# A third level of the seven-product scheme, in one of the seven inner products, in a two-layer LoRA kernel

## Chip, cores and metric

The kernel runs on one core of one Trainium2 chip. The metric is the device time in microseconds of one execution of the whole program. The time before the change is 521.71 us, the median of three runs (521.3 to 521.96).

## The reference, cut to what matters

All arrays are float32. `x` has 64 requests of 64 tokens with 1024 features, 4096 tokens in all.

```python
# layer 0: a rank-16 adapter per request, added to x
Bx  = einsum('bni,bri->bnr', x, B0[ids0])
x   = x + einsum('bnr,bor->bno', Bx, A0[ids0])
# layer 1: a dense 1024 x 1024 product and eight gated adapters of rank 16, added to x
base   = einsum('btd,od->bto', x, W)
logits = einsum('btd,ed->bte', x, Wr) + 5.0 * one_hot(ids1)
gates  = softmax over the two largest logits, zero elsewhere
h      = einsum('btd,erd->bter', x, A1)
x      = x + base + 2.0 * einsum('bter,bte,eor->bto', h, gates, B1)
```

Nearly all the arithmetic is `base`, the product of 4096 tokens with the 1024 x 1024 matrix `W`. The `x +` of layer 1 is folded into it, as an identity added to `W`.

## The kernel before

**Layout and stages.** Features lie on the partitions, tokens along the free axis. The 4096 tokens are eight blocks of 512 (`TB`), worked off as four pairs (`NSUP`; the pair is called `s`, 0 to 3). For each block there are a few small TensorE stages: transposes of gathered adapter rows (`pt`), the projection to rank 16 (`project`, tile `pb` written from `x,bt`), the rank-16 update of x (`adapt`, tiles `px`, added to x on VectorE), the adapters and router logits (`rows`, tile `ph`, 128 x 136 per matmul), the gates (VectorE) and a transpose of the gated rows (`pg`, line 609). The rest is the dense product.

**The dense product** (`products`, line 817) is done twice over with the Strassen-Winograd scheme, which gets a 2 x 2 by 2 x 2 block product from seven block products instead of eight, at the price of sums of blocks. The outer level takes the two feature halves, the two output halves and the two token blocks of a pair: seven outer products, n = 1, 2, 6, 7, 5, 3, 4 in that order (`ORDER`, line 251). The inner level splits each outer product (512 features, 512 outputs, 512 tokens) again into seven inner products k = 1 to 7, each of 256 features, 256 outputs and 256 tokens. One inner product is four matmul instructions of 128 x 128 weights and 256 tokens (`product`, line 876): two output halves, each summed over two feature halves. In n = 2, 3, 7 and 4, four of the inner products (k = 2, 3, 7, 4) carry two more matmuls, which add the gated adapters from `b1_sb`. Only outer product 1 of pair 0 is done without the inner split (`WHOLE`, tile `pw`).

**Operands.** For pair 0 the weight sums of the inner level are made by GpSimd (`weights`, line 700) and written to DRAM (`s_kept`); the pairs 1 to 3 read all seven weight tiles of an outer product back through SP's queue, into the rotating SBUF pool `"s"` of 28 tiles, 256 KB each. Token sums of the outer level are made by VectorE (`token_sum`, line 736), those of the inner level by GpSimd in pairs 1 to 3 (`inner_tokens`, line 758).

**PSUM and leaving it.** Pools `"a"` and `"b"` have two banks each, `"l"` four. Products 1, 6, 5 and 3 of an outer product add up in one bank `pa`, 7 and 4 in one bank `pb2`, and product 2 is alone in a bank `pc` of pool `"b"` (all shown as `pb` in the profile). `leave` (line 909) takes a bank out after each step, while the sum goes on in it: VectorE adds it to the output tile, or ScalarE copies it where there is nothing to add. So a later step into the same bank waits for the `leave` of the step ahead of it.

**Order of the work.** Inside `products` each outer product does `step(n, 1)`, the left-over steps 3 and 4 of the outer product before it in between, `step(n, 2)`, then `begin` of the next outer product, then 6, 7 and 5. Each operation is a step of a planner (`Plan`, line 34) with a cost on its engine, a due time `at`, what it reads and writes and which pool slots it takes. The planner lists the steps in time once, when the program is built, and each engine runs its own list strictly in that order, with semaphores between engines. All instructions go out through one wrapper, so the profile shows line 29 for nearly all of them, and groups are told apart by tile names.

Of the kernel before, what the change touches and what calls it, by code (L numbers as in the profile page):

```python
# [8 lines left out]
F32 = mybir.dt.float32  # L9
I32 = mybir.dt.int32  # L10
AF = mybir.ActivationFunctionType
ALU = mybir.AluOpType
AX = mybir.AxisListType

P = 128
# [166 lines left out]
def kernel(  # L182
# [59 lines left out]
    QC = NC // 4  # L242
    QO = O // 4
    HT = TB // 2
# [8 lines left out]

    WHOLE = {(0, 1)}

    pe, dve = Pinned(tc, nc.tensor), Pinned(tc, nc.vector)
    act, pool, sp = Pinned(tc, nc.scalar), Pinned(tc, nc.gpsimd), Pinned(tc, nc.sync)
    engine = {"DVE": dve, "POOL": pool}

    slots = {  # L260
        "q": 7, "s": 28, "t5": 2, "t6": 2, "t7": 2, "t4": 2, "o": 3, "hg": 3, "hd": 3,
        "gb": 2, "ga": 2, "bt": 1, "bx": 1, "h": 1, "l": 4, "a": 2, "b": 2,
    }
    plan = Plan(slots, {"l"})
# [7 lines left out]
    def new(tag, shape, name):  # L272
        return pools[tag].tile(shape, F32, tag=tag, name=name)
# [36 lines left out]
    b1_sb = const.tile([P, O], F32, name="b1_sb")  # L310
# [44 lines left out]
    made = {}  # L355

    def part(t, cs=range(HC), gs=range(NG)):
        return [(t, c, g) for c in cs for g in gs]
# [302 lines left out]
    }  # L661
    m_q = {1: quarter[0, 0], 2: quarter[0, 1], 4: quarter[1, 1]}
    s_kept = tc.dram_tile([7, 7, P, QC * QO], F32, name="s_kept")

    def combine(out, a, b, op, at, engines):

# [9 lines left out]
    DVE = {"DVE": 0.62}  # L676
    POOL = {"POOL": 1.25}
# [20 lines left out]
    wt, ti = {}, {}  # L698

    def weights(s, n, at):  # L700

        out = {}
        if s > 0:
            for i, m in enumerate(ORDER):
                out[m] = t = ("s", s, n, m)

                def fn(e, t=t, m=m):
                    made[t] = new("s", [P, QC, QO], f"s_{s}_{n}{m}")
                    sp.dma_start(made[t].rearrange("p c o -> p (c o)"), s_kept[n - 1, m - 1])

                plan.add({"SP": 0.1}, fn, [("kept", n, m)], [(t,)], at + i - 8, [("s", t)], kb=256)
            wt[n] = out
            return
        m = m_q[n]
        out = {1: m[0, 0], 2: m[0, 1], 4: m[1, 1]}
        for k, (u, v, op) in {
            5: ((1, 0), (1, 1), ALU.add),
            6: (5, (0, 0), ALU.subtract),
            7: ((0, 0), (1, 0), ALU.subtract),
            3: ((0, 1), 6, ALU.subtract),  # L720
        }.items():
            out[k] = ("s", s, n, k)
            uu = m[u] if isinstance(u, tuple) else out[u]
            vv = m[v] if isinstance(v, tuple) else out[v]
            combine(out[k], uu, vv, op, at - 4, POOL)
        for k in ORDER:
            t = out[k]

            def keep(e, t=t, k=k):
                sp.dma_start(s_kept[n - 1, k - 1], made[t].rearrange("p c o -> p (c o)"))  # L730

            plan.add({"SP": 0.1}, keep, [(t,)], [("kept", n, k)], at + 4, kb=256)
        wt[n] = out


    def token_sum(s, n, at):
# [21 lines left out]
    def inner_tokens(s, n, m, at):  # L758
        def b(i, j):
            return made[m][:, i * QC : (i + 1) * QC, j * HT : (j + 1) * HT]  # L760

        def keys(i, j):
            return part(m, range(i * QC, (i + 1) * QC), range(2 * j, 2 * j + 2))

        out = {k: (("view", i, j), keys(i, j)) for k, i, j in ((1, 0, 0), (2, 1, 0), (3, 1, 1))}
        for k, u, v in ((5, (0, 1), (0, 0)), (6, (1, 1), 5), (7, (1, 1), (0, 1)), (4, (1, 0), 6)):
            t = ("ti", s, n, k)

            def fn(e, t=t, k=k, u=u, v=v):
                made[t] = new(f"t{k}", [P, QC, HT], f"ti_{s}_{n}{k}")  # L770
                vv = b(*v) if isinstance(v, tuple) else made["ti", s, n, v]
                engine[e].tensor_tensor(made[t], b(*u), vv, ALU.subtract)

            vk = keys(*v) if isinstance(v, tuple) else [(("ti", s, n, v),)]
            plan.add(
                POOL if s else DVE, fn, keys(*u) + vk, [(t,)], at - 5,
                [(f"t{k}", t)], sb=True,
            )
            out[k] = (t, [(t,)])
        ti[n] = {  # L780
            k: ((lambda t=t: b(*t[1:])) if t[0] == "view" else (lambda t=t: made[t]), ks)
            for k, (t, ks) in out.items()
        }
# [33 lines left out]
    def products(s):  # L817
        ka, kb = 2 * s, 2 * s + 1
        slot = [0]
        hd, dest, banks, left = {}, {1: "U", 6: "U", 7: "V"}, {}, {}  # L820
# [7 lines left out]
        def at():  # L828
            return s * SLOTS + slot[0]
# [5 lines left out]
        def q(d, i, cs, js):  # L835
            t = made[d][i] if isinstance(d, str) else made["o", s, d, i]
            return t[:, cs[0] : cs[-1] + 1, js[0] * HT : (js[-1] + 1) * HT]

        def qk(d, i, cs, js):
            return [(name(d, i), c, j) for c in cs for j in js]  # L840

        ALL = (0, 1)
# [66 lines left out]
        def leave(n, ps, i, cs, js, more=False):  # L909
# [22 lines left out]
                [("o", name(d, i))] * fresh,  # L932
            )

        def done(n, i, cs, js):

            if n == 5:

                p5, u, v = (lambda d=d: q(d, i, cs, js) for d in (5, "U", "V"))
                k5, ku, kv = (qk(d, i, cs, js) for d in (5, "U", "V"))  # L940
                plan.add(
                    DVE, lambda e: dve.tensor_tensor(u(), u(), p5(), ALU.add), ku + k5, ku,
                    at() - 2, sb=True,
                )
                plan.add(
                    DVE, lambda e: dve.tensor_tensor(p5(), v(), p5(), ALU.add), kv + k5, k5,
                    at() - 2, sb=True,
                )
            oh, k = {2: (0, ka), 5: (1, kb), 3: (0, kb), 4: (1, ka)}.get(n, (None, None))
            if oh is None:  # L950
                return
            o0 = (oh * 2 + i) * QO
            if last(n):


                def some(e):
                    t0, r0 = k * TB + js[0] * HT, o0 + cs[0] * P
                    sp.dma_start(
                        outT[r0 : r0 + len(cs) * P, t0 : t0 + HT].rearrange("(c p) t -> p c t", p=P),
                        q(n, i, cs, js),  # L960
                    )

                plan.add({"SP": 0.1}, some, qk(n, i, cs, js), [], at() + 2, kb=128 * len(cs))
                return
            left[n, i] = left.get((n, i), 2) - 1
            if left[n, i] == 0:

                def store(e):
                    sp.dma_start(
                        outT[o0 : o0 + QO, k * TB : (k + 1) * TB].rearrange("(c p) t -> p c t", p=P),  # L970
                        made["o", s, n, i],
                    )

                plan.add({"SP": 0.1}, store, qk(n, i, ALL, ALL), [], at() + 2, kb=512)

        def begin(n):
            dest.setdefault(n, n)
            if s == 0 and n in (6, 3):
                outer(n, at() - 4)
            weights(s, n, at() + (6 if (s, n) in WHOLE else 0))  # L980
            if s == 0 and n == 2:
                outer(5, at() + 4)
                outer(7, at() + 8)
            if (s, n) in WHOLE:
                whole_h[n] = {2: ("hg", ka), 3: ("hg", kb), 7: ("hg", kb), 4: ("he", s)}.get(n)
                if n == 4:
                    gate_diff(s, at() - 2)
                return
            inner_tokens(s, n, tokens[n], at())
            if n == 4:  # L990
                gate_diff(s, at() - 2)
            if n in (2, 7, 3, 4):
                gate_sum(s, n, hd, at() - 2)
# [34 lines left out]
        for n in ORDER:  # L1028
            after = ORDER[ORDER.index(n) + 1] if n != ORDER[-1] else None
            if (s, n) in WHOLE:  # L1030
                for k in rest:
                    step(*k)
                rest = []
                for x in range(4):
                    whole_product(n, x // 2, x % 2)
                    if x == 1 and after is not None:
                        begin(after)
                continue
            step(n, 1)
            if rest:  # L1040
                step(*rest[0])
            step(n, 2)
            if rest:
                step(*rest[1])
            if after is not None:
                begin(after)
            step(n, 6)
            step(n, 7)
            step(n, 5)
            rest = [(n, 4), (n, 3)] if last(n) else [(n, 3), (n, 4)]  # L1050
        for k in rest:
            step(*k)
# [89 lines left out]
```

## Time and profile before

| | |
|---|---|
| median of three runs | 521.71 us (521.3 to 521.96) |
| the profiled execution, its own time | 521.43 us |
| span of that execution in the profile | 519.6 us |
| granted TensorE clock, mean | 1.0 |
| ScalarE copy `h<-ph`, 272 columns, x16 | 386 ns each |
| ScalarE copy `o<-pa`, 512 columns, x16 | 586 ns each |
| VectorE `bx<-pb,mask`, 128 columns, x8 | 286 ns each |
| VectorE `hd<-hg`, 256 columns, x8 | 420 ns each |
| VectorE `o<-pb,o`, 512 columns, x47 | 690 ns each |
| GpSimd `ti<-x`, 512 columns, x24 | 1283 ns each |
| DMA, mean over the span | 191 GB/s, 99.19 MB in packets |

Times in the profile count from the start of the span. PE is TensorE's matmul row and PEld its weight loads, which overlap it. A float32 matmul instruction stands as two records, each with a weight load of its own: the 256 instructions of `ph` (8 blocks, 4 strips, 8 chunks) are 512 records. A transpose is one record. The length of a record includes the pipeline's fill and drain, so the rate of a run of matmuls is read from start to start, not from the mean length. A timeline line gives start, length, engine, line, operation, output<-inputs, shape, how many records in a row, and in brackets how long the engine idled before it and what released it.

### The profile page before, as it was taken

Reading aid. Unit: us, or ns where it says so; the run is one execution under the profiler, and the core shown is the slowest. Engines: PE = TensorE matmul, PEld = TensorE weight load, DVE = VectorE, ACT = ScalarE, POOL = GpSimd, SP = SyncE. Lnnn points to the kernel's source line nnn. Section 1 sums busy time; section 2 is a strip of 40 time slices with the busy share of each in tenths; the row PEclk is TensorE's granted clock in tenths of the full one; section 3 lists DMA queues with packets and bytes.
Section 4 is the critical chain, followed back from the end, with each engine's and each line's share of the span. In section 5 each row is a group of like instructions: output and inputs, shape, how many; then the busy total and the mean of one; then the engine's idle time right before and its main releaser. Section 6 shows DMA issues by size and latency. Waiting matters only on the chain.

```text
span 519.6 us, 8547 instructions
## 1 busy us (share of the span) xinstructions
PE 505.6 (97%) x3432; PEld 439.8 (85%) x3432; DVE 301.2 (58%) x574; ACT 41.0 (8%) x81; POOL 170.2 (33%) x141
## 2 busy tenths in 40 slices
PE   2999999999999999999999999999999999999997
PEld 2857988888888988898888998889888898888886
DVE  0689998986853383616693256345576417433633
ACT  1111100002000100012000100000200010000000
POOL 4073058180332144123243313311423322433300
PEclk9999999999999999999999999999999999999999
DMA  7999275799666259726575536743546634620122
GB/s 263 371 368 400 78 262 216 272 326 350 199 187 218 61 179 317 242 74 204 165 241 168 177 86 214 266 166 109 174 163 199 203 88 112 208 65 0 42 101 101
DMA packets 54263, 99.19 MB, mean 191 GB/s; under 512 B 4944, under 2 KB 11088, under 8 KB 54224
## 3 DMA queue, kind: packets, MB, share of 16 engines
q1 hardware_dynamic: 51920, 90.26, 52.3%
q0 software_dynamic: 2304, 8.39, 4.6%
q8 instruction: 27, 0.44, 0.3%
q14 instruction: 12, 0.10, 0.0%
HBM read 69.01 MB, written 29.62 MB: 190 GB/s over the span
## 4 chain that ended last, share of the span: by engine, by line
PE 97%; DMA 2%; DVE 0%; issue 0%; SPq 0%; POOL 0%
PE pa L29 39%; PE pb L29 38%; PE ph L29 11%; PE px L29 3%; PE pw L29 3%; DMA x<-in_xT 2%; PE pt L29 1%; PE pg L29 1%; DVE o L29 0%; SPq L29 0%; DVE bx L29 0%; POOL x L29 0%
## 5 line engine op out<-in xcount | busy, mean ns | idle before, releaser
L29 PE MATMUL pa<-ti,s 128*128 128x256 f32 x432 | 102.5, 380 | 0.0
L29 PE MATMUL pb<-ti,s 128*128 128x256 f32 x384 | 95.8, 380 | 0.0
L29 PEld LDWEIGHTS pa<-ti,s 128*128 128x128 f32 x432 | 80.8, 190 | 11.2 <-issue 0.2
L29 PEld LDWEIGHTS pb<-ti,s 128*128 128x128 f32 x384 | 72.1, 190 | 10.0
L29 PEld LDWEIGHTS ph<-a_sb,x 128*128 128x128 f32 x512 | 62.6, 190 | 1.5 <-issue 0.4
L29 PE MATMUL ph<-a_sb,x 128*128 128x136 f32 x512 | 63.1, 279 | 0.2 <-issue 0.2
L29 POOL TENSOR_TENSOR ti<-x,ti 128x512 f32<-128x512 f32 x24 | 32.2, 1340 | 78.0 <-PE pb L29 77.1
L29 DVE TENSOR_TENSOR o<-pb,o 128x512 f32<-128x512 f32 x47 | 32.4, 690 | 35.5 <-PE pb L29 21.1
L29 PE MATMUL pa<-x,s 128*128 128x256 f32 x216 | 51.9, 379 | 0.0
L29 POOL TENSOR_TENSOR ti<-t,ti 128x512 f32<-128x512 f32 x18 | 25.7, 1429 | 71.0 <-PE pb L29 61.3
L29 POOL TENSOR_TENSOR ti<-x 128x512 f32<-128x512 f32 x24 | 30.8, 1283 | 55.3 <-PE pb L29 41.8
L29 PEld LDWEIGHTS pa<-x,s 128*128 128x128 f32 x216 | 40.1, 190 | 5.3 <-issue 0.3
L29 DVE TENSOR_TENSOR x<-px,x 128x512 f32<-128x512 f32 x64 | 39.8, 682 | 7.2 <-PE px L29 7.2
L29 PE MATMUL pa<-t,s 128*128 128x256 f32 x168 | 41.0, 380 | 0.0
L29 POOL TENSOR_TENSOR ti<-t 128x512 f32<-128x512 f32 x18 | 24.4, 1357 | 42.9 <-PE pb L29 33.4
L29 PEld LDWEIGHTS pa<-t,s 128*128 128x128 f32 x168 | 31.6, 190 | 4.5 <-issue 0.4
L29 DVE TENSOR_TENSOR o<-pa,u 128x512 f32<-128x512 f32 x32 | 22.0, 688 | 20.7 <-PE pa L29 20.1
L29 POOL TENSOR_TENSOR s<-w,w 128x512 f32<-128x512 f32 x12 | 17.2, 1434 | 36.3 <-DVE w L29 36.3
L29 DVE TENSOR_TENSOR u<-pb,u 128x512 f32<-128x512 f32 x21 | 14.5, 689 | 25.1 <-ACT u L29 20.7
L29 PE MATMUL pb<-hg,b_sb 128*128 128x256 f32 x96 | 28.6, 379 | 0.0
L29 DVE TENSOR_TENSOR o<-pa,v 128x512 f32<-128x512 f32 x15 | 10.3, 689 | 24.0 <-PE pa L29 24.0
L29 DVE TENSOR_TENSOR v<-pa,u 128x512 f32<-128x512 f32 x16 | 11.0, 689 | 22.3 <-PE pa L29 22.1
(113 smaller groups left out, 611.0 us busy)
## 6 DMA issues: line engine op xcount, KB each, us to landing
s<-s_kept SPq DMA_DIRECT2D x147, 256.0 KB
x<-in_xT SPq DMA_DIRECT2D x15, 1024.0 KB
out_T<-o SPq DMA_DIRECT2D x30, 512.0 KB
s_kept<-s SPq DMA_DIRECT2D x28, 256.0 KB
s_kept<-w SPq DMA_DIRECT2D x18, 256.0 KB
w<-in_w SPq DMA_DIRECT2D x16, 256.0 KB
x<-in_xT SPq DMA_DIRECT2D x2, 512.0 KB
s_kept<-m SPq DMA_DIRECT2D x3, 256.0 KB
```

What stands on the lines that cost most here:

```text
L29: return self._tc.keep_in_program_order(f(*args, **kwargs))
```

## The change

From pair 1 on (`FINE = 1`), inner product k = 2 of every outer product is split a third time, by the same scheme: its 256 x 256 weights into four blocks of 128 x 128, its 256 tokens into two groups of 128. In place of four matmuls of 128 x 128 weights and 256 tokens there are seven of 128 x 128 weights and 128 tokens, in four parts. The first part does four of them, one into each quarter of the bank; the other three parts do one each, adding into the second quarter, and lie ahead of the steps 6, 7 and 5. Between the parts ScalarE copies the running second quarter into a new SBUF tile `cp` (after the first part, the fourth quarter as well). After the last part VectorE takes the bank out as before and makes three more additions, from `cp`.

The scheme needs sums of weight blocks (tile `sf`: four GpSimd operations of 128 columns per outer product in pair 1, kept in DRAM as `f_kept`, loaded by SP in pairs 2 and 3) and of token blocks (tile `tt`: three VectorE operations per outer product). Pool `"s"` goes from 28 tiles to 26 and now also holds `sf`. The two matmuls for the gated adapters stay as they are, behind the last part. Pair 0 does as before.

```diff
+    FINE = 1
-        "q": 7, "s": 28, "t5": 2, "t6": 2, "t7": 2, "t4": 2, "o": 3, "hg": 3, "hd": 3,
+        "q": 7, "s": 26, "tt": 2, "cp": 2, "t5": 2, "t6": 2, "t7": 2, "t4": 2, "o": 3, "hg": 3, "hd": 3,
+    f_kept = tc.dram_tile([7, P, QC * QO], F32, name="f_kept")
...
+    def fine_weights(s, n, a, at):
...
+            v.tensor_tensor(f[:, 0], a21, a22, ALU.add)
+            v.tensor_tensor(f[:, 1], f[:, 0], a11, ALU.subtract)
+            v.tensor_tensor(f[:, 2], a11, a21, ALU.subtract)
+            v.tensor_tensor(f[:, 3], a12, f[:, 1], ALU.subtract)
...
+        if s == FINE:
+            plan.add({"POOL": 1.6}, sums, [(a,)], [(t,)], at - 3, [("s", t)], sb=True)
+            plan.add({"SP": 0.1}, keep, [(t,)], [("fine", n)], at + 4, kb=256)
+        else:
+            plan.add({"SP": 0.1}, load, [("fine", n)], [(t,)], at - 6, [("s", t)], kb=256)
...
+        def begin_fine(n):
...
+                dve.tensor_tensor(
+                    f[:, :2], b[:, :, P:], b[:, 0, :].rearrange("p (h t) -> p h t", t=P), ALU.subtract
+                )
+                dve.tensor_tensor(f[:, 2], f[:, 1], b11, ALU.add)
+                dve.tensor_tensor(f[:, 3], b21, f[:, 2], ALU.subtract)
...
+        def fine_product(n, part_):
...
+                todo = [
+                    [(1, a11, b11), (0, a12, b21), (3, s3, t3), (2, a22, t4)],
+                    [(1, s2, t2)],
+                    [(1, s1, t1)],
+                    [(1, s4, b22)],
+                ][part_]
+                for x, (c, lhs, rhs) in enumerate(todo):
+                    pe.matmul(
+                        out[:, c], lhs, rhs, start=(part_ == 0 and x == 0), stop=True,
+                        skip_group_check=True,
+                    )
...
+            def copy(e):
...
+                    act.copy(made[cp][:, 0::3], out[:, 1::2])
+                else:
+                    act.copy(made[cp][:, part_], out[:, 1])
...
+            leave(n, ps, 0, ALL, (0,), True)
...
+            def rest_(e):
+                o, c = q(dest[n], 0, ALL, (0,)), made[cp]
+                c11, c21, c2 = o[:, 0, :P], o[:, 1, :P], o[:, 1]
+                dve.tensor_tensor(c11, c11, c[:, 0], ALU.add)
+                dve.tensor_tensor(c2, c2, c[:, 1:3].rearrange("p h t -> p (h t)"), ALU.add)
+                dve.tensor_tensor(c21, c21, c[:, 3], ALU.add)
...
-            step(n, 2)
+            if s >= FINE:
+                fine_product(n, 0)
+            else:
+                step(n, 2)
...
-            step(n, 6)
-            step(n, 7)
-            step(n, 5)
+
+            for x, k in enumerate((6, 7, 5)):
+                if s >= FINE:
+                    fine_product(n, 1 + x)
+                if s >= FINE and x == 2:
+                    done(n, 0, ALL, (0,))
+                step(n, k)
```

More of the change, by code (lines that the diff above doesn't have):

```diff
@@ L712, in weights @@
             wt[n] = out
+            if s >= FINE:
+                fine_weights(s, n, out[2], at)
             return
@@ L733, in weights, with blocks, load, sums @@
         wt[n] = out
+    def fine_weights(s, n, a, at):
+        t = ("sf", s, n)
+        def blocks():
+            made[t] = new("s", [P, QC, QO], f"sf_{s}_{n}")
+            return made[t].rearrange("p c (o w) -> p (c o) w", w=P)
+        def load(e):
+            blocks()
+            sp.dma_start(made[t].rearrange("p c o -> p (c o)"), f_kept[n - 1])
+        def sums(e):
+            f, w4 = blocks(), made[a].rearrange("p c (o w) -> p (c o) w", w=P)
+            a11, a21, a12, a22 = (w4[:, x] for x in range(4))
+            v = engine[e]
+            v.tensor_tensor(f[:, 0], a21, a22, ALU.add)
+            v.tensor_tensor(f[:, 1], f[:, 0], a11, ALU.subtract)
+            v.tensor_tensor(f[:, 2], a11, a21, ALU.subtract)
+            v.tensor_tensor(f[:, 3], a12, f[:, 1], ALU.subtract)
+        def keep(e):
+            sp.dma_start(f_kept[n - 1], made[t].rearrange("p c o -> p (c o)"))
+        if s == FINE:
[3 more added lines that the diff above has]
+            plan.add({"SP": 0.1}, load, [("fine", n)], [(t,)], at - 6, [("s", t)], kb=256)
+        wt[n]["fine"] = t
     def token_sum(s, n, at):
@@ L933, in leave, with fn @@
             )
+        fine = {}
+        def begin_fine(n):
+            t, (tx, tk) = ("tt", s, n), ti[n][2]
+            def fn(e):
+                made[t] = new("tt", [P, 4, P], f"tt_{s}_{n}")
+                f, b = made[t], tx()
+                b11, b21 = b[:, 0, :P], b[:, 1, :P]
+                dve.tensor_tensor(
[3 more added lines that the diff above has]
+                dve.tensor_tensor(f[:, 3], b21, f[:, 2], ALU.subtract)
+            plan.add({"DVE": 0.9}, fn, tk, [(t,)], at() - 3, [("tt", t)], sb=True)
@@ new lines, in fine_product, with fn @@
+        def fine_product(n, part_):
+            ps, cp = ("pc", s, n), ("cp", s, n)
+            a, f, t, (tx, tk) = wt[n][2], wt[n]["fine"], ("tt", s, n), ti[n][2]
+            extra = hd[n][2] if n in (2, 3, 7, 4) and part_ == 3 else None
+            oh = {2: 0, 3: 0, 7: 1, 4: 1}.get(n)
+            def fn(e):
+                if part_ == 0:
+                    made[ps] = new("b", [P, QC, HT], f"pf_{s}_{n}")
+                out = made[ps].rearrange("p o (h t) -> p (o h) t", t=P)
+                w4 = made[a].rearrange("p c (o w) -> p (c o) w", w=P)
+                a11, a21, a12, a22 = (w4[:, x] for x in range(4))
+                s1, s2, s3, s4 = (made[f].rearrange("p c (o w) -> p (c o) w", w=P)[:, x] for x in range(4))
+                b4 = tx()
+                b11, b21, b22 = b4[:, 0, :P], b4[:, 1, :P], b4[:, 1, P:]
+                t1, t3, t2, t4 = (made[t][:, x] for x in range(4))
+                todo = [
[9 more added lines that the diff above has]
+                    )
+                if extra is not None:
+                    for j in range(QC):
+                        o = oh * 2 * QC + j
+                        pe.matmul(
+                            made[ps][:, j], b1_sb[:, o * P : (o + 1) * P], extra[0](),
+                            start=False, stop=True, skip_group_check=True,
+                        )
+            reads = [(a,), (f,), (t,)] + tk + ([("b1",), extra[1]] if extra is not None else [])
+            plan.add(
+                {"PE": (0.88, 0.22, 0.22, 0.22)[part_] + 0.86 * (extra is not None)}, fn, reads,
+                [(ps,)], at(), [("b", ps)] * (part_ == 0),
+            )
+            slot[0] += (0.5, 0.13, 0.13, 0.13)[part_]
+            def copy(e):
+                out = made[ps].rearrange("p o (h t) -> p (o h) t", t=P)
+                if part_ == 0:
+                    made[cp] = new("cp", [P, 4, P], f"cp_{s}_{n}")
+                    act.copy(made[cp][:, 0::3], out[:, 1::2])
+                else:
+                    act.copy(made[cp][:, part_], out[:, 1])
+            if part_ < 3:
+                plan.add(
+                    {"ACT": 0.45 if part_ == 0 else 0.3}, copy, [(ps,)] + [(cp,)] * (part_ > 0),
+                    [(cp,)], at() - 4, [("cp", cp)] * (part_ == 0),
+                )
+                return
+            leave(n, ps, 0, ALL, (0,), True)
+            region = qk(dest[n], 0, ALL, (0,))
+            def rest_(e):
[4 more added lines that the diff above has]
+                dve.tensor_tensor(c21, c21, c[:, 3], ALU.add)
+            plan.add({"DVE": 0.9}, rest_, [(cp,)] + region, region, at() - 4, sb=True)
@@ L989, in begin @@
             inner_tokens(s, n, tokens[n], at())
+            if s >= FINE:
+                begin_fine(n)
             if n == 4:
@@ L1041, in products @@
                 step(*rest[0])
-            step(n, 2)
+            if s >= FINE:
+                fine_product(n, 0)
+            else:
+                step(n, 2)
             if rest:
@@ L1046, in products @@
                 begin(after)
-            step(n, 6)
-            step(n, 7)
-            step(n, 5)
+            for x, k in enumerate((6, 7, 5)):
+                if s >= FINE:
+                    fine_product(n, 1 + x)
+                if s >= FINE and x == 2:
+                    done(n, 0, ALL, (0,))
+                step(n, k)
             rest = [(n, 4), (n, 3)] if last(n) else [(n, 3), (n, 4)]
```

## Prediction

> **What bounds the kernel.** I read the busy table of the page first, then what the matmul engine waited for, then the timeline of a few stretches, to get rates from start to start.
>
> ```profile
> PE 505.6 (97%) x3432; PEld 439.8 (85%) x3432; DVE 301.2 (58%) x574; ACT 41.0 (8%) x81; POOL 170.2 (33%) x141
> ```
>
> ```profile
> PE pt L29 <- DMA gb<-in_b,idx: 9.8, 1, 9.8
> PE px L29 <- DVE bx L29: 0.4, 1, 0.4
> PE pb L29 <- DMA x<-in_xT: 0.2, 1, 0.2
> PE ph L29 <- issue: 0.2, 1, 0.2
> ```
>
> The second view lists all waits of PE (total, times, longest). After the first 9.8 us PE lost 0.8 us in the whole span. So the end is set by TensorE, and a change is worth the matmul time it removes, less the waits it opens. The rates come from these lines (start, length, ..., records in the run):
>
> ```profile
> 201.70 1.04 PE L29 MATMUL pt<-ident,gb 128*128 128x128 f32 x8
> 202.57 1.89 PE L29 MATMUL pa<-ti,s 128*128 128x256 f32 x8
> 204.30 1.89 PE L29 MATMUL pa<-t,s 128*128 128x256 f32 x8
> 206.12 1.96 PE L29 MATMUL pb<-x,bt 128*32 128x128 f32 x64
> 208.00 1.99 PE L29 MATMUL pa<-t,s 128*128 128x256 f32 x8
> 209.93 0.39 PE L29 MATMUL px<-bx,ga 32*128 32x128 f32 x4
> ```
>
> ```profile
> 218.48 2.02 PE L29 MATMUL ph<-a_sb,x 128*128 128x136 f32 x16
> 220.33 1.03 PE L29 MATMUL pb<-ti,s 128*128 128x256 f32 x4
> ```
>
> From 202.57 to 204.30 eight records of 256 columns take 1.73 us, 0.216 each. From 218.48 to 220.33 sixteen of 136 columns take 1.85, 0.1156 each. From 201.70 to 202.57 eight of 128 take 0.87, 0.109 each, every one with its own weights. The clock is 1.0 throughout.
>
> **TensorE's work.** There are 3 pairs x 7 outer products = 21 changed inner products. Each loses 4 matmuls of 256 tokens, 8 records: 8 x 0.216 = 1.73 us. Each gains 7 of 128 tokens, 14 records. No row shows a float32 product (two records per instruction) with 128 moving columns. The near rows are `pt`, same shape and a fresh weight load per record but a transpose (0.109), and `ph`, a true product with eight columns more (0.1156). The first gives 14 x 0.109 = 1.53, a gain of 0.20; the second 14 x 0.1156 = 1.62, a gain of 0.11. Fewer columns can hardly be slower than more, so `ph` is the upper bound. I take 0.109, because 0.216 at 256 and 0.1156 at 136 lie on a line that gives 0.109 at 128. The sum: 21 x 0.20 = 4.2 us off the path, at worst 21 x 0.11 = 2.3.
>
> A rule of the Trainium skill speaks against this. "TensorE: Matmul & The Clock Gate", section "Back-to-back issue gap", puts a sustained stream of load and matmul pairs at about 81 ns per matmul for 128 columns, where the bare formula gives 56: 1.45 times as long, because the weight load counts too. Carried over to these records that is 0.158 each, 14 x 0.158 = 2.21 us per product, a loss of 0.48 each and 10 us in all. The rows say otherwise: `pt` and `ph` are such streams, and keep to the straight line of the long matmuls. I go by the rows.
>
> **Matmuls beside the change.** As built, the projection of one block in pair 1 is cut in two by a 256-column step, so PE turns once more from and to the small-tile form. That costs what 204.30 to 206.12 (1.82) and 208.00 to 209.93 (1.93) have over 1.73: 0.09 and 0.20, the second a way in plus a way out. So +0.2 us.
>
> **The new waits of PE.** Parts two to four wait for ScalarE's copy of the part ahead. A copy begins about 0.2 us after the last matmul's slot and takes 0.27 us for 128 columns or 0.37 for 256 (by the line through 386 ns at 272 and 586 at 512). So 0.5 to 0.6 us. In the built order the matmul work between parts is 1.73 us or more at 61 of 63 places and 0.87 at two (a set of transposes). Covered; without cover each would cost 0.6, so 38 us if nothing lay between. ScalarE is strictly in order, and one or two 0.59 us copies ahead of it make 1.8: just the cover. Its load grows from 41 us by 21 x (0.37 + 0.27 + 0.27) = 19, to 12%.
>
> The planner also moves neighbours. At four places (outer product 1 of pairs 2 and 3, 5 and 3 of pair 3) a step that adds into `pa` now has only part one, 0.87 us, between it and the step ahead, whose bank must be taken out first. The nearest case of before is
>
> ```profile
> 493.62 1.89 PE L29 MATMUL pa<-ti,s 128*128 128x256 f32 x8
> 495.35 1.89 PE L29 MATMUL pa<-t,s 128*128 128x256 f32 x8
> 495.55 0.69 DVE L29 TENSOR_TENSOR o<-pa,u 128x512 f32<-128x512 f32 x1 [2.73 <-PE pa L29]
> 497.08 1.03 PE L29 MATMUL pa<-x,s 128*128 128x256 f32 x4
> ```
>
> The step of 493.62 ends its slot at 495.35, VectorE is done at 496.24, and PE comes back at 497.08: 0.84 spare of 1.73, so the round trip is 0.89. Against 0.87 it is barely late, and a weight load that could not run ahead adds 0.1 (the 208.00 line has one). I put 0.15 each, 0.6 in all; between 0 and 2 if VectorE or ScalarE is also late.
>
> **VectorE, off the path.** Each product adds three operations for `tt` and three after the last part: columns 256, 128, 128 twice, so 2 x (0.42 + 0.29 + 0.29) = 2.0 us. Slowed by GpSimd at the same time, as in
>
> ```profile
> 483.14 1.77 POOL L29 TENSOR_TENSOR ti<-t,ti 128x512 f32<-128x512 f32 x1
> 484.29 1.16 DVE L29 TENSOR_TENSOR o<-v,o 128x512 f32<-128x512 f32 x1
> ```
>
> (1.16 for 0.69), it is 3.4. GpSimd is busy a third of the time, so 2.4, 50 us in all, 301 to 351 (68%). What is queued behind: the three additions stand ahead of the `leave` after step 5, and step 3 waits for that. From the end of part four VectorE needs 0.2 + 0.69 for the bank, 1.0 to 1.7 for the additions and 0.69 for the `leave`: 2.6 to 3.3. PE gives it step 5 (1.73) plus, in the built order, 2.3 us or more (one step and a `pt` or `ph` set), or, in outer product 3 of pair 3, step 1 ahead of step 5: 4.0 or more. Covered, at no cost, as long as VectorE isn't more than 0.7 behind.
>
> **GpSimd and DMA.** 28 GpSimd operations of 128 columns, a quarter of 1.28 plus a start, some 0.5 us each: 14 us in pair 1, beside its 33%. Token sums queued behind a wait for `sf`'s operands are due an outer product later, some 18 us. DMA gains 14 loads and 7 stores of 256 KB, 5.5 MB on 99. Set against each tile's first matmul, its load was issued 42 us ahead or more; 26 tiles at 8 per product hold 3.25 products for 4 before, which takes 0.75 x 18 = 13 us from that. Still 29. In pair 0 PE's order is unchanged; the two missing tiles make GpSimd's sums wait for earlier steps of PE, which in the trace end before those sums began. No cost.
>
> **Sum.** 521.43 - 4.2 + 0.2 + 0.6 = 518.0 for an execution like the profiled one. The median stood 0.3 higher: 518.3.
>
> **Rivals.**
> - *Loads bind.* Short matmuls run at 0.1156: 521.7 - 2.3 + 0.2 + 0.6 = 520.2. For it: loads fill 85% of the span already, and no true product of 128 columns is shown. Against: the straight line and `pt`. Chance, with other half-eaten gains (a late copy here and there): 0.14.
> - *Copies eat it.* ScalarE's copies come late behind others, 0.2 us per product: 21 x 0.2 = 4.2, so 521.7 + 0.2 = 521.9. Against: 1.73 cover for 0.6. Chance of no change 0.09.
> - *Slower: VectorE falls behind.* Its stretch from 370 to 405 is busy 23.3 of 35 us; two products add 4 to 7, so 27 to 30 of 35, in strict order with `leave` behind the additions. Where it runs more than the 0.7 to 0.8 spare late, PE stands. It decides from 0.2 us of wait per product; at 0.35 it is 21 x 0.35 - 4.2 = +3.2, 525. Against: PE never waited for VectorE in that stretch before, and the spare grew at most places. Chance 0.15.
> - *The split isn't made*: the built order has 147 matmuls of 128 x 128 x 128 in place of 84; none left.
>
> **Numbers.** The forecast case (517.3 to 519.3) has 0.62. 0.2%, about what a measurement of this kernel can tell from no change, is 1.04 us: faster is below 520.7, so 0.62 + 0.14 = 0.76; same 0.09; slower 0.15. The range goes from 517.2 (no new wait at all) to 522.0, which takes in the half-eaten and the eaten gain and leaves out 0.15 and little more.
>
> **What would show it.** Right: `pf` records 0.109 apart within part one; PE's list of waits grown by under 1.5 us; busy PE shorter by about 4; VectorE near 350 busy. Wrong: 0.115 or more between `pf` records (loads bind); PE or PEld waits on ACT `cp` (copies); PE waits on DVE `o`, `u` or `v` of several us between 240 and 410 (VectorE behind); a load `s` or `sf` that PE waits for.

## The result and the profile after

The changed kernel takes 519.24 us (median of six runs, 518.82 to 520.08), the kernel before 521.52 beside it. The ratio is 0.9957, with a 95% interval of 0.9944 to 0.9970: faster, by 2.3 us. The forecast was 3.4 us below the median of before (518.3). The profiled execution, the fastest of the six, has an own time of 518.82 us and a span of 517.0; before they were 521.43 and 519.6.

The busy table of the page after:

```profile
PE 502.6 (97%) x3558; PEld 441.3 (85%) x3558; DVE 359.2 (69%) x700; ACT 59.1 (11%) x144; POOL 183.8 (36%) x169
```

PE is 3.0 us shorter, with 126 records more. ScalarE has 18 us more (19 forecast), GpSimd 13.6 (14), VectorE 58 (50). DMA moved 104.73 MB, 5.5 more, as forecast. TensorE's list of waits after (in total, times, longest):

```profile
PE pt L29 <- DMA gb<-in_b,idx: 9.8, 1, 9.8
PE px L29 <- DVE bx L29: 0.4, 1, 0.4
PE pb L29 <- DMA x<-in_xT: 0.3, 1, 0.3
PE ph L29 <- issue: 0.2, 1, 0.2
```

It has the four lines of before and no new one. That isn't the whole story: a record of 256 columns is 0.38 us long and its slot 0.216, so a gap of 0.1 us between two slots doesn't show as idle time, and the one of 0.30 us below isn't in the list either. The small waits of this case are read from start to start. From the first `pw` matmul to the last matmul of the kernel TensorE needed 487.31 us before and 484.95 after, 2.36 less. The first `pw` itself came 0.38 us earlier in this execution, in a stretch that the change doesn't touch.

This is a first part of the new product (timeline of TensorE, after):

```profile
233.83 0.61 PE L29 MATMUL pf<-x,s 128*128 128x128 f32 x4
234.27 0.39 PE L29 MATMUL pf<-tt,sf 128*128 128x128 f32 x2
234.49 0.39 PE L29 MATMUL pf<-tt,s 128*128 128x128 f32 x2
234.72 1.03 PE L29 MATMUL pb<-ti,s 128*128 128x256 f32 x4
```

Eight records from 233.83 to 234.72 are 0.111 us each. Over all `pf` records of 128 columns, the places with a wait or a turn to or from small tiles left out, it is 109 to 112 ns, 111.0 on the mean: the first record of a matmul 110.4, the second 111.7. The forecast took 109.

And this is a wait that the forecast did not have (all engines, after, outer product 4 of pair 1):

```profile
271.91 2.36 DVE L29 TENSOR_TENSOR t<-t,x 128x512 f32<-128x512 f32 x2
...
272.34 1.38 POOL L29 TENSOR_TENSOR ti<-x,ti 128x512 f32<-128x512 f32 x1 [6.41 <-PE pb L29]
...
274.20 0.68 DVE L29 TENSOR_TENSOR o<-pb,o 128x512 f32<-128x512 f32 x1
...
274.41 0.38 PE L29 MATMUL pf<-tt,sf 128*128 128x128 f32 x2
...
274.93 0.73 PEld L29 LDWEIGHTS pb<-ti,s 128*128 128x128 f32 x4 [0.32 <-DVE o L29]
```

VectorE takes 2.36 us for two token sums. The first takes 0.60; the second, begun at 272.51 while GpSimd's operation is under way (272.34 to 273.72), takes 1.76. Only then does VectorE take out a bank of pool `"b"` (274.20 to 274.88). Step 7 needs that bank. Its first matmul could have begun at 274.63, behind the two records of `pf`; it begins at 274.93. With 0.10 more in its second record, that is 0.40 us.

### The profile page after: what moved, and what is told of

The parts are those of the page before. It is cut to its first block, busy times and chain, and to the rows that moved or that the text cites. A ratio compares the mean times of both kernels' runs of the same rounds, so it can differ in the third digit from the quotient of the medians.

```text
span 517.0 us, 9064 instructions
## 1 busy us (share of the span) xinstructions
PE 502.6 (97%) x3558; PEld 441.3 (85%) x3558; DVE 359.2 (69%) x700; ACT 59.1 (11%) x144; POOL 183.8 (36%) x169
## 2 busy tenths in 40 slices
DMA packets 57290, 104.73 MB, mean 203 GB/s; under 512 B 5280, under 2 KB 11424, under 8 KB 57248
## 4 chain that ended last, share of the span: by engine, by line
PE 92%; DVE 3%; DMA 2%; issue 1%; POOL 1%; SPq 0%; POOLq 0%
PE pa L29 37%; PE pb L29 28%; PE ph L29 11%; PE pf L29 8%; PE px L29 3%; PE pw L29 3%; DMA x<-in_xT 2%; DVE o L29 1%; PE pt L29 1%; DVE t L29 1%; PE pg L29 1%; POOL ti L29 0%; DVE x L29 0%; DVE tt L29 0%; SPq L29 0%
## 5 line engine op out<-in xcount | busy, mean ns | idle before, releaser
L29 PE MATMUL pb<-ti,s 128*128 128x256 f32 x384 | 95.7, 380 | 0.1
L29 PEld LDWEIGHTS pa<-ti,s 128*128 128x128 f32 x432 | 79.4, 190 | 10.0 <-issue 0.2
L29 PEld LDWEIGHTS pb<-ti,s 128*128 128x128 f32 x384 | 70.5, 190 | 8.7 <-DVE o L29 0.3
L29 POOL TENSOR_TENSOR ti<-x,ti 128x512 f32<-128x512 f32 x24 | 32.2, 1340 | 71.6 <-PE pb L29 70.7
L29 ACT COPY cp<-pf 128x128 f32<-128x128 f32 (+1 forms) x63 | 19.0, 302 | 182.4 <-PE pf L29 161.8
L29 DVE TENSOR_TENSOR o<-pb,o 128x512 f32<-128x512 f32 x35 | 24.1, 689 | 13.6 <-PE pb L29 12.8
L29 PE MATMUL pf<-tt,sf 128*128 128x128 f32 x126 | 24.6, 277 | 0.0
L29 PEld LDWEIGHTS pf<-tt,sf 128*128 128x128 f32 x126 | 21.7, 191 | 2.1
L29 DVE TENSOR_TENSOR x<-x,x 128x512 f32<-128x512 f32 x16 | 12.5, 798 | 12.6 <-PE ph L29 12.6
```

What stands on the lines that cost most here:

```text
L29: return self._tc.keep_in_program_order(f(*args, **kwargs))
```

## The experiments

The theory (A) that this profile suggests: the gain is the matmul time removed, as forecast, but a float32 record with 128 weight columns doesn't come faster than about 111 to 112 ns, whatever the tokens, because its weights must be loaded; the rest that is missing are small waits for VectorE. The rivals: the records cost what their moving columns cost and the loss is elsewhere (copies, VectorE, tiles); or the floor is a fixed cost per record (theory B of quarters).

**halves64.** Each of the seven matmuls is cut into two of 64 tokens.

```diff
-                    pe.matmul(
-                        out[:, c], lhs, rhs, start=(part_ == 0 and x == 0), stop=True,
+                    for g in range(2):
+                        pe.matmul(
+                            out[:, c, g * 64 : (g + 1) * 64], lhs, rhs[:, g * 64 : (g + 1) * 64],
...
```

> Each of the 147 matmuls of 128 tokens is cut in two of 64 tokens with the same weights, so there are 588 pf records of 64 columns in place of 294 of 128. In the changed kernel a pf record takes 111.7 ns from start to start, 2.5 more than a transpose of the same shape. Theory A, the weight load of a true float32 product is what takes 111.7: a record of 64 columns takes 111.7 as well, 294 x 0.1117 = +33 us, about 552. Theory B, the columns take it, with some 5 ns added per record: a record takes 53 + 5 = 58 ns, 588 x 0.058 = 34.1 against 32.8, +1.3 us, about 520.5. In between (80 to 100 ns) the load is partly hidden.

Measured: 551.62 us, ratio 1.0582 (1.0562 to 1.0601). The span is 549.2. The 294 added records cost 32.2 us of span, 0.110 each. TensorE's timeline:

```profile
215.11 0.61 PE L29 MATMUL pf<-tt,sf 128*128 128x64 f32 x4
215.56 0.61 PE L29 MATMUL pf<-tt,s 128*128 128x64 f32 x4
```

Four records of 64 tokens from 215.11 to 215.56 are 0.112 each, as long as with 128 tokens. (The first record of a part often takes 0.056, and then the second record of the matmul behind the part comes 0.056 late, so the part as a whole pays 0.112 per record.) So the tokens don't set it: at 128 weight columns there is a floor of 0.112 per record. This run alone doesn't tell a load of the weights from a fixed cost per record.

**no_vector.** The six VectorE operations are left out (`tt` is a constant tile, the additions from `cp` are not made), with TensorE's order as in the change.

```diff
-                dve.tensor_tensor(f[:, 2], f[:, 1], b11, ALU.add)
-                dve.tensor_tensor(f[:, 3], b21, f[:, 2], ALU.subtract)
+                made[t] = tt_c
...
-                dve.tensor_tensor(c11, c11, c[:, 0], ALU.add)
-                dve.tensor_tensor(c2, c2, c[:, 1:3].rearrange("p h t -> p (h t)"), ALU.add)
-                dve.tensor_tensor(c21, c21, c[:, 3], ALU.add)
+                pass
```

> The changed kernel in the same built order, without the six VectorE operations per outer product: the token sums are a constant tile, filled once, and the three additions after the last part are left out (so the pairs 1 to 3 are not the product). ScalarE's copies stay. Theory A, the rate of the records is the larger part of what is missing to 4.2 us and VectorE's lateness only some 0.5: 518.8, ratio to before 0.995; the wait of 0.4 at step 7 of outer product 4 of pair 1 goes, the ones of 0.07 at three places stay, VectorE busy falls from 359 to about 310. Theory B, VectorE's 58 us more cost over 1 us in waits: 518.0 or less, 0.9935 or less.

Measured: 518.88 us, ratio 0.9954 (0.9941 to 0.9968), not to be told apart from the changed kernel. VectorE is busy 299.2 us, and the wait at 274.9 is gone. From the first `pw` to the last matmul it is 484.72 us. That is 0.23 below the changed kernel: 0.40 for the wait that is gone, less 0.18 for one at a small-tile set at 208.4. So VectorE's added work makes the one wait and little else.

**no_copies.** ScalarE's copies are left out (`cp` is a constant tile).

```diff
-                    act.copy(made[cp][:, 0::3], out[:, 1::2])
-                else:
-                    act.copy(made[cp][:, part_], out[:, 1])
+                    made[cp] = tt_c
```

> The changed kernel in the same built order, without ScalarE's 63 copies: the parts two to four wait for nothing, and VectorE adds a constant tile instead (so the pairs 1 to 3 are not the product). Theory A, the copies are covered by the step between the parts: 519.2, no change from the changed kernel, ratio to before 0.9957. Theory B, the copies or the reads of a bank that PE goes on writing cost PE: 518.5 or less, and pf records in the single parts start earlier.

Measured: 519.29 us, ratio 0.9965 (0.9952 to 0.9979). No gain: the copies are covered. The waits of step 7 of outer product 4 stand here too, 0.29 and 0.30 us in pairs 1 and 2.

**slots26.** The kernel before, with 26 tiles in pool `"s"` (one number changed).

> The kernel before with 26 tiles in the pool of weights in place of 28, and nothing else; TensorE's built order stays. Theory A, the prefetch lead of 42 us or more covers it: no change, 521.5, ratio 1.000. Theory B, the smaller pool costs a part of what is missing to 4.2 us: 522 or more, with PE or GpSimd waits on weight tiles that the kernel before doesn't have.

Measured: 521.26 us, ratio 1.0003 (0.9995 to 1.0011). The two tiles cost nothing.

**quarters.** As halves64, and each matmul also cut into two of 64 weight columns, all with 64 tokens.

```diff
-                for x, (c, lhs, rhs) in enumerate(todo):
...
+                for h in range(2):
+                    for x, (c, lhs, rhs) in enumerate(todo):
+                        for g in range(2):
+                            pe.matmul(
+                                out[h * 64 : (h + 1) * 64, c, g * 64 : (g + 1) * 64],
+                                lhs[:, h * 64 : (h + 1) * 64], rhs[:, g * 64 : (g + 1) * 64],
...
```

> As halves64, but each of those matmuls is also cut in two by weight columns (64 weights columns, 64 tokens), with the two halves of the weights not taken in turn. 1176 pf records in place of halves64's 588, which took 111.7 ns each whatever their columns. Theory A, that time is the load of the weights and goes with their columns: a record takes half of it, about 56 ns, 1176 x 0.056 = 65.7 us as in halves64, about 552. Theory B, it is a fixed price of a load-and-matmul pair: 1176 x 0.1117 = 131.4, about 617. Less than 552 would mean that the two column halves of the array overlap.

Measured: 564.21 us, ratio 1.0830 (1.0785 to 1.0876), between the two expectations, for a reason that neither had. TensorE's timeline:

```profile
243.61 0.46 PE L29 MATMUL pf<-x,s 128*64 128x64 f32 x5
243.90 0.40 PE L29 MATMUL pf<-tt,sf 128*64 128x64 f32 x4
244.13 0.40 PE L29 MATMUL pf<-tt,s 128*64 128x64 f32 x4
244.46 0.91 PE L29 MATMUL pb<-ti,s 128*128 128x256 f32 x3
```

Within one half of the weight columns a record takes 0.058 us (0.29 for five, 0.23 for four). With the weight columns halved as well, the floor of 0.112 is gone: by the line of the moving columns 64 tokens alone would give 0.056. That falls against a fixed cost per record. What made the time longer is the turn into and out of the smaller weight form: 93 ns into it, 94 out of it (the last line: 0.33 where 0.23 would do), and 104 more in the second record after it, 0.29 per part. Over 84 parts that is 24 us, and some 22.5 without what nine parts behind a small-tile stage would have paid in any case. The 1176 records take 0.047 on the mean, because the two column halves overlap where one follows the other: 55 us for 32.6. The sum is 22.5 + 55 - 32.6 = 45 us, and the span grew by 44.1.

**pair3_only.** The change in pair 3 alone.

```diff
-    FINE = 1
+    FINE = 3
```

> The split from pair 3 on alone (FINE = 3), where no gates and token stages lie between. 7 products at 8 x 0.2157 - 14 x 0.1117 = 0.162 us: 1.13 us, less two short waits of pair 3 (0.07 and 0.16): 0.9 us. Theory A, the gain is the same per product in each pair: a third of the whole, ratio 0.9983. Theory B, the split loses in pairs 1 and 2, where VectorE is fuller, and the gain sits in pair 3: 1.5 us or more, 0.997 or less.

Measured: 520.68 us, ratio 0.9996 (0.9984 to 1.0009); by the time of the whole kernel this can't be told from no change, and the expected ratio, 0.9983, lies just outside the interval. In the trace the stretch from the first `pw` to the last matmul is 486.37 us, 0.94 below before; a third of the changed kernel's 2.36 is 0.79. So the stretch is in keeping with a gain per product. The time doesn't show it in part because this kernel spends more outside the profiled span: 2.15 us (time less span, median of its 14 executions), where the kernel before has 1.77. Why is not known; by the spans alone it is 0.45 us shorter (518.55 for 519.0).

**changed_again.** The changed kernel once more.

> The changed kernel once more beside the others, to have it on the same chip: ratio 0.9957 as before if the gain holds.

Measured: 519.15 us against 520.73, ratio 0.9967 (0.9958 to 0.9975). The gain is 1.6 us here. In this trace the wait of step 7 of outer product 4 stands in pair 1 and in pair 2 (0.30 and 0.29 us, each with 0.10 behind it), and a small-tile set at 208.3 waits 0.16. The first profile of the changed kernel was one with fewer of these waits than usual.

**pool_adds_lag.** The three additions from `cp` on GpSimd, and the planner's allowance between engines raised.

```diff
-    LAG = 0.2
+    LAG = 0.35
...
-                dve.tensor_tensor(c11, c11, c[:, 0], ALU.add)
+                pool.tensor_tensor(c11, c11, c[:, 0], ALU.add)
...
-            plan.add({"DVE": 0.9}, rest_, [(cp,)] + region, region, at() - 4, sb=True)
+            plan.add({"POOL": 1.7}, rest_, [(cp,)] + region, region, at() - 4, sb=True)
```

> The changed kernel with the three additions after the last part on GpSimd in place of VectorE, and the planner's allowance between engines 0.35 us in place of 0.2, which takes the four 0.87 us places out of the built order. Theory A, those four places (0.37 us) and the late VectorE at one place (0.40) are all the waits there are: 0.7 us less than the changed kernel, 518.0 to 518.5 where the changed one is 519. Theory B, GpSimd's two-input additions come later and hold up step 3 or the token sums, or the other order costs elsewhere: the changed kernel's time or more.

Measured: 523.84 us, ratio 1.0061 (1.0035 to 1.0087): slower, so the expectation failed. Two things were changed at once, and the next two runs take them apart.

**pool_adds.** The additions on GpSimd alone (the diff above without its first two lines).

> The changed kernel with its three additions after the last part on GpSimd in place of VectorE; the planner's allowance between engines stays 0.2. Theory A (what the last run with GpSimd lost came from the larger allowance, which alters the order of pair 0 too): VectorE is some 20 us less busy, the waits of 0.3 us for VectorE in outer product 4 are gone, and the time is that of the changed kernel or up to 0.4 us less, 518.6 to 519.3, ratio 0.995 to 0.9972. Theory B (GpSimd does the additions late and TensorE stands for them): 521 or more, ratio 1.0005 or more, with waits of TensorE on `o`, `u` or `v` close to 1 us.

Measured: 517.76 us against 520.93, ratio 0.9940 (0.9926 to 0.9953), below what either theory expected. VectorE is busy 338.9 us, GpSimd 217.8. A stretch of the same outer product 4 of pair 1:

```profile
270.37 0.69 DVE L29 TENSOR_TENSOR o<-pb,o 128x512 f32<-128x512 f32 x1 [0.31 <-PE pb L29]
...
272.11 0.38 PE L29 MATMUL pf<-tt,sf 128*128 128x128 f32 x2
...
272.33 1.03 PE L29 MATMUL pb<-ti,s 128*128 128x256 f32 x4
```

VectorE was idle when the bank came due, and took it out at once; step 7 starts 0.22 us after the two records of `pf` began, with no gap. The waits of the changed kernel are gone but two of 0.16 and 0.07 us. This version beats both kernels. It isn't a change of one thing: with other costs the planner also gave TensorE another order at several places, one of them just ahead of this stretch.

**lag_only.** The raised allowance alone (the first two lines of that diff).

> The changed kernel with the planner's allowance between engines at 0.35 in place of 0.2, the additions on VectorE as in the change. Theory A (the order that the allowance gives to pair 0 costs the time): TensorE comes to its first `pw` matmul some 3 us later after its own first matmul than in the changed kernel, 522 to 524, ratio 1.002 to 1.0065. Theory B (GpSimd's additions cost it): as the changed kernel, 519.0 to 519.6, ratio 0.9965 to 0.998.

Measured: 523.25 us, ratio 1.0037 (1.0022 to 1.0051). The allowance alone makes it slow. TensorE's timeline, and the table of busy times for the stretch from 16.6 to 20.0 us (its last three numbers are the granted clock, the DMA share and GB/s):

```profile
16.12 0.72 PE L29 MATMUL pt<-ident,gb 128*128 128x128 f32 x4 [2.04 <-DMA gb<-in_b,idx]
16.77 3.58 PE L29 MATMUL px<-bx,ga 32*128 32x128 f32 x64
```

```profile
16.60:20.00 3.40, 3.40 (x62) 3.23 (x64) 1.06 (x2) 0.59 (x1) 0.00 (x0) 0.50 1.06 390
```

The planner put a set of transposes ahead of the rank-16 update in pair 0, and TensorE stands 2.04 us for its gathered rows. Half a us behind that wait the granted clock falls to 0.50 for 3.4 us, and is 1.00 before and after; the 64 records of `px` take 3.58 us in it, for 2.07 in changed_third. From the first matmul of the kernel to the first `pw` it takes 22.17 us, for 18.47 in changed_third beside it: 3.7 us lost in a stretch that the change never touched, 1.5 of them by the clock. It doesn't fall in every execution: the two with a mean granted clock of 1.0 take 522.21 and 522.49 us, the three with 0.996 or 0.997 take 523.25 to 524.0. That the wait brings it on is not shown. Behind the first `pw` it is another 1.6 us longer than changed_third: TensorE waits 0.59, 0.19, 0.54 and 0.65 us (at 64.8, 69.5, 95.7 and 212.2), where changed_third has 0.18 and 0.19 at two of these places and nothing at the others.

**changed_third.** The changed kernel on the same chip as these two.

> The changed kernel again, on the same chip as the two runs beside it, so that differences of some tenths of a us can be read: 519.2, ratio 0.9965. Its trace shows how far the small waits for VectorE in outer product 4 (0.3 us each, in one or both of pairs 1 and 2) differ between executions.

Measured: 519.41 us, ratio 0.9970 (0.9957 to 0.9982). The wait of step 7 stands in both pairs again (0.30 each). pool_adds lies 1.65 us below it, and their intervals do not overlap. In the traces the stretch from the first `pw` to the last matmul is 485.51 us here and 484.41 in pool_adds: 1.1 less, as much as the waits differ by (1.36 and 0.23). Another 0.4 lies ahead of the first `pw`, where nothing was changed.

## Why the prediction was right, and by what it was off

The sign and the mechanism were right: matmul time is taken off a path that is TensorE's nearly alone. The gain forecast was 3.4 us; 2.3 came. By its terms, in the profiled execution:

- **TensorE's work, -4.2: mis-sized.** It measured -3.6. The step that failed is "I take 0.109, because 0.216 at 256 and 0.1156 at 136 lie on a line that gives 0.109 at 128". The line of the moving columns holds down to 136, but a record with 128 weight columns has a floor that lies just above it at 128: 111.0 ns on the mean, 0.6 us over the 294 records. halves64 shows the floor (0.112 with half the tokens), quarters that it falls with the weight columns (0.058 with half of those). That the load of the weights sets it is what these two leave, and is not measured by itself. The transposes of `pt` misled here: they come at 109, and their weight loads are shorter, as these lines show (weight loads of after; busy us, mean ns | idle before).

```profile
L29 PEld LDWEIGHTS pt<-ident,gb 128*128 128x128 f32 x64 | 7.9, 152 | 10.2 <-issue 9.8 <-DVE x L29 0.2
L29 PEld LDWEIGHTS pf<-tt,sf 128*128 128x128 f32 x126 | 21.7, 191 | 2.1
```

- **The rival "loads bind" (520.2)** had the mechanism that came, at a fraction of its price: 111.0, not 115.6. That `ph` is an upper bound held.
- **The estimate from the Trainium skill** ("TensorE: Matmul & The Clock Gate", section "Back-to-back issue gap": 81 ns per matmul for 56 by the bare formula), rejected: right. The records took 1.02 times the line, not 1.45.
- **One more turn to small tiles, +0.2: mis-sized.** The turn cost what was forecast, 93 ns into it and 104 in the second record behind it. But the projection that it cuts in two also became longer. In one piece it took 1.88 us (206.12 to 208.00, before); now each half takes 1.01, as these lines show for the first (after). Together +0.34.

```profile
205.25 1.08 PE L29 MATMUL pb<-x,bt 128*32 128x128 f32 x32
206.26 1.99 PE L29 MATMUL pa<-t,s 128*128 128x256 f32 x8
```

- **Four places of 0.87 us, +0.6:** they cost something, less than taken: 0.07 us at three (283.3, 407.5, 468.2) and 0.16 at the fourth, 0.37 in all. The fourth, after, in the timeline:

```profile
494.35 0.61 PE L29 MATMUL pf<-t,s 128*128 128x128 f32 x4
494.55 0.69 DVE L29 TENSOR_TENSOR o<-pa,u 128x512 f32<-128x512 f32 x1 [1.03 <-PE pa L29]
...
495.30 1.13 PE L29 MATMUL pa<-x,s 128*128 128x256 f32 x4
```

  Eight records of the first part end their slots 0.89 us after 494.35, at 495.24; the bank is out at 495.24 too, and the next step starts at 495.30: 0.06 late, and 0.10 in its second record.

- **VectorE, no cost: wrong at one place.** The step was "Covered, at no cost, as long as VectorE isn't more than 0.7 behind". It reckoned with the `leave` after step 5 alone. The bank of pool `"b"` that step 7 of outer product 4 takes over was left out, and it costs 0.40 us, once in this execution and twice in the other two profiled ones of the changed kernel. no_vector shows that the wait comes from VectorE's added work: it is gone there, with TensorE's order unchanged. The load was also under-estimated, 58 us for 50. The forecast read the pair at 483.14 and 484.29 as VectorE running 1.7 times slower beside GpSimd. It is a hold, not a slower rate: that operation ended at 485.45, 0.54 us after GpSimd's. A 128-column operation of the change, after:

```profile
226.05 1.44 POOL L29 TENSOR_TENSOR ti<-x 128x512 f32<-128x512 f32 x1 [5.68 <-PE pa L29]
226.40 1.24 DVE L29 TENSOR_TENSOR tt<-tt,x 128x128 f32<-128x128 f32 x1
```

  It takes 1.24 us for the 0.29 of its kind elsewhere, and ends 0.15 after GpSimd's (227.49). In this trace 61 of the 63 two-input operations of VectorE with both inputs in SBUF and 128, 256 or 512 columns that began while one of GpSimd was under way end 0.15, 0.28 or 0.55 us after it, by their columns. Those that take a PSUM bank out (an input in PSUM, 512 columns) keep their 0.68 beside GpSimd. So a short operation can lose 1 us, several times its own length, and the second token sum ahead of the late bank (273.72 and 274.27) is such a case. The rival of 525 needed 0.2 us of wait per product to decide; 0.40 once or twice over 21 products is 0.02 to 0.04.
- **Copies covered, tiles and DMA free:** right, by no_copies and slots26.

The sum as measured: -3.6 + 0.34 + 0.37 + 0.40 = -2.5. The stretch from the first `pw` gives -2.36; what is between them are slots of 256 columns that come a few ns late (0.13). In executions where the wait of step 7 stands twice, with one more at a small-tile set, the same stretch gives -1.8, which is what the later ratios show.

That pool_adds is faster than the changed kernel has two parts, which the runs separate in size but not by one change each: the 0.4 us waits, which go with VectorE's load alone (no_vector), though here TensorE's order near them is another one too, and three of the 0.07 us places, which go because the planner's order has other work there.

## What to carry to other kernels

When matmuls are cut finer, compare moving columns with weight columns: in these runs the record's rate followed the larger of the two (64 weight columns with more tokens was not run), so a split that ends at 128 tokens on 128 weight columns still gains nearly in full (0.17 of 0.20 us per product), and fewer tokens per record than that gain nothing more (halves64). Where a step's cover is cut, list every PSUM bank that is handed over within that stretch, not only the one that the change touches, and read small waits of TensorE from start to start, since the view of waits doesn't show them. Before VectorE is given small additions between SBUF tiles, see what GpSimd runs at that time: each may be held until GpSimd's operation ends. A planner's setting that is raised to help one place reorders all others; try it alone.

## What the runs showed of the hardware that was not expected

- A float32 record with 128 weight columns took 111 to 112 ns with 128 tokens and with 64; with 64 weight columns and 64 tokens 58.
- A turn of TensorE to weights of 64 columns costs 93 ns into it, 94 out of it, and 104 more in the second record behind it, 0.29 us in all (quarters). The turn to `px`, weights of 32 rows, has the same 93 and 104, before and after.
- A VectorE operation on two SBUF inputs that began while a two-input operation of GpSimd was under way ended a fixed time after it, 0.15 us at 128 columns and 0.55 at 512 (61 of 63 cases, after); one with an input in PSUM wasn't held.
- GpSimd did the additions from `cp` to `o` in 0.50 us at 128 columns and 0.81 at 256 (pool_adds). VectorE's means, 0.49 and 0.42 (after), mix free and held ones: of the 24 of 128 columns 17 took 0.29 and four 1.24 to 1.32.
- In lag_only and pool_adds_lag the granted clock was 0.50 for one stretch of 3.4 us in pair 0, where a set of transposes had waited for its rows; the other traces don't have it there.
